# A four-layer convolution chain on one core: order of the set-up, one background task, and the final output by columns

## The chip, the cores and the metric

The kernel runs on one core of a Trainium2 chip. A core has a matrix engine (TensorE, PE in the profile), a vector engine (VectorE, DVE), a scalar engine (ScalarE, ACT), a general engine (GpSimd, POOL) and a synchronising engine (SyncE, SP). [...] Data moves between DRAM and on-chip memory by DMA; SP, ACT and POOL issue the transfers, and 16 DMA engines carry them. The metric is the time of one execution on the device in microseconds (us); less is better.

## What is computed

The input x is 1024 samples of 16 x 16 x 16 values (height, width, channels). Four layers follow, each as x + layer(groupnorm(x)):

```python
x = x + _L0_conv_ref(_gn(x), core0, core1, core2)        # one 4096 x 4096 matrix, given by three small cores
x = x + _L1_conv_ref(_gn(x), ...)                        # cellular automaton step: 3x3 depthwise, 48->128->16, mask
x = x + _L2_conv_ref(_gn(x), filters, bias)              # 3x3 convolution
x = x + _L3_conv_ref(_gn(x), ...)                        # cellular automaton step again
```

`_gn` normalises over 8 groups of two channels. In layer 0 the cores are of the form (r, o, i, k); their contraction is the matrix that is applied to each sample. In layers 1 and 3 every pixel goes through 48 -> 128 (relu) -> 16, and a mask from a 3 x 3 maximum of one channel decides what is kept.

## The kernel before

The samples are handled in two chunks of 512 (NB = 512, NCH = 2). Two large on-chip tiles, `XN[0]` and `XN[1]`, hold a chunk each, or parts and scratch rooms. The order of instructions on every engine is the order in which the Python code makes them: nothing is rescheduled.

**Layer 0** is a train of 13 stages (`phases[0]` to `phases[12]`), about 107 us each, with four units of work each. Before its first unit can start, set-up must do the following; all of it stands in the last part of `conv_preact_kernel`, from L2041 on.

- `train_setup` (from L587) loads the cores and copies core 0 into a widened tile `c0r` (L619, DVE). `sums` (L621) turns that on PE into `A`, and `coefs(0)` makes `R` of it on DVE. `cores` (L631) turns core 1 with PE into the tiles convw and pack.
- `early` (L662) makes the first part of a product g with 64 small matmuls (L644), copies it with ACT (L672) and stores it to DRAM. `keep_g` (L648) issues the stores: two of them in one layout (`g_dram[0]`, L651), and four in another (`g_dram[1]`, L658). `early` calls it for q = 0 and q = 1, all on POOL's queue.
- `gload(0, 1)` and `gload(0, 0)` (L1422, its DMA at L1438) fetch g back for the first unit, from `g_dram[0]` of q = 0. `build(0, 1)` and `build(0, 0)` (L1442) multiply g with R (L1459) and copy the result with ACT (L1464): these are the weights of the first unit. `mix` (L1489) adds halves of them on DVE.
- `input_steps` (from L1053): 8 loads of the input chunk on SP (L1074), statistics on DVE (`stats`, L1086, and `aggregate`, L1116), transposes on PE (L1092) with copies by ACT (L1096, L1098), then `tail`: `root` (L1119, and a square root on ACT, L1120), `widen(0)` (the mean widened by four copies, L1134), `newton` (L1124 to L1128), `widen(1)`. `spread0` and `spread1` turn the widened tiles on PE and copy them with ACT (L1143).
- `kept(0)` and `kept(1)` (L1145) store the turned input to DRAM on POOL (L1151 and L1148).
- `first_normed` (L1176) applies mean and scale to a quarter of the part; `x00`, `x11`, `x10`, `x01` are its four operations each, at L1174. `x00` reads from a tile `raw`; `x11` and `x10` overwrite the tile that `kept(1)` stores. `combined` (L1186, its operations at L1203) makes sums of them.

[...]

**Work beside the train.** `run` places background steps among the pieces of a stage: a span (steps, lo, hi) says from which to which share of the stage. `aside` lists them: stage 7 has `set3`, the preparation of layer 3's weights, with the bound 0.85. Its last steps store a scratch room in `XN[0]` to DRAM (L328 to L330), and the room is written again by the sums for stage 8 (L1203).

**The last layer** of the last chunk is `layer_nca` with `xo`. For every quarter q of the channels and every pair of columns w2 it does matmuls (L1974), relu on ACT (L1977), matmuls (L1803), then `finish` and `residual` on DVE (L1815, L1855, L1860), and after a few slots `turn` (L1864), which transposes on PE (L1867) and copies into `xo` with DVE (L156). At q = 3 the last two column pairs are done in two halves of the samples (hf 0 and 1). SP fetches, two units ahead, the weights `wq` (L1754) and the residual `res` (L1777); for the last pairs their place in SP's order is after the turn of (3, 3). When (q, w2) = (3, 7) is turned, for each half, four stores of 1 MB leave on SP (L1882). Beside it `output_steps(0)` writes the first chunk's output (L1360, L1371).

Of the kernel before, what the change touches and what calls it, by code (L numbers as in the profile page):

```python
# [20 lines left out]
B, S, C = 1024, 16, 16  # L21
P = 128
NB = 512
# [82 lines left out]
def conv_preact_kernel(ctx: ExitStack, tc: tile.TileContext, a: dict, out: bass.AP):  # L106
    nc = tc.nc
# [25 lines left out]
    def work(shape, tag, name, dt=F32):  # L133
        p, sizes = pool["sb"]
        return p.tile(shape, dt, tag=tag, name=name, bufs=sizes[tag])
# [454 lines left out]
    def train_setup(room):  # L590

        c1s = room[:, 0:1024].rearrange("p (h x r k) -> p h x r k", h=2, x=4, r=4)
        c1t = [t[:, 0:512].rearrange("p (x m) -> p x m", x=4) for t in (convw, pack)]
        c1n = work([P, 2, NB], "t4", "core1")[:, :, 0:256]
        r = work([P, NB], "n", "cores")
        c2 = r[:, 0:256]
        c0n = r[:, 256:288].rearrange("p (t k) -> p t k", t=2)

        c0r = work([P, NB], "s", "core0")[:, 0:256].rearrange("p (t n k) -> p t n k", t=2, n=8)
        nc.sync.dma_start(
            c0n, a["L0_conv_core0"].rearrange("r o i k -> (r o i) k").rearrange("(t p) k -> p t k", p=P)
        )
        for g in range(4):
            nc.sync.dma_start(
                c2[32 * g : 32 * g + 16], a["L0_conv_core2"].rearrange("r o i k -> r (o i k)")
            )
        core1 = a["L0_conv_core1"].rearrange("k o i q -> o k (i q)")
        for wv in range(4):  # L610
            for a2 in range(2):
                r0 = 64 * (wv // 2) + 32 * a2 + wv % 2
                (A if wv < 2 else G).dma_start(
                    c1n[r0 : r0 + 31 : 2],
                    core1[8 * a2 + wv : 8 * a2 + wv + 5 : 4].rearrange("h k f -> k h f"),
                )
        G.memset(room[:, 0:1024], 0.0)
        for t in range(2):
            V.tensor_copy(c0r[:, t], c0n[:, t].unsqueeze(1).broadcast_to([P, 8, S]))  # L619

        def sums():  # L621

            t = st0["A"] = work([P, 2, P], "A", "A")
            pt = bank([P, 2, P], "o", "pc0")
            for e in range(2):
                T.transpose(pt[:, e], c0r[:, e].rearrange("p n k -> p (n k)"), ident)
            pt = pt.rearrange("p e (o b i) -> p b i e o", b=2, i=8)
            for b in range(2):
                A.copy(t[:, b].rearrange("p (i e o) -> p i e o", e=2, o=8), pt[:, b])

        def cores():  # L631
            for h in range(2):
                G.tensor_copy(
                    c1s[:, h, :, :, 0:16], c1n[:, h].rearrange("p (x r k) -> p x r k", x=4, r=4)
                )
            for h in range(2):
                pt = bank([P, 4, P], "o", "pc1")
                for x in range(4):
                    T.transpose(pt[:, x], c1s[:, h, x].rearrange("p r k -> p (r k)"), ident)
                A.copy(c1t[h], pt)  # L640

        def gmul(pg, h, ih, x, r, q):
            rows = slice(32 * r, 32 * r + 16)
            T.matmul(  # L644
                pg, c1t[h][rows, 2 * ih + x], c2[rows, 64 * q : 64 * q + 64], start=True, stop=True
            )

        def keep_g(h, q, g, queue):  # L648

            for w in range(2):  # L650
                queue.dma_start(  # L651
                    g_dram[0][h, q, w].rearrange("o s k (t f) -> (s k t) o f", t=2),
                    g[64 * w : 64 * w + 64],
                )
            for w in range(2):
                for v in range(2):
                    rows = slice(64 * w + 32 * v, 64 * w + 32 * v + 32)
                    queue.dma_start(  # L658
                        g_dram[1][v, q, w, :, h].rearrange("o k (t f) -> (k t) o f", t=2), g[rows]
                    )  # L660

        def early():  # L662

            g = work([P, 2, 8, P], "w0", "gw")
            pg = [bank([P, 2, 4, 64], "w", "pg") for _ in range(4)]
            for x in range(2):
                for k in range(4):
                    for r in range(4):
                        gmul(pg[r][:, x, k], 0, k % 2, x, r, k // 2)
            for q, x, r in product(range(2), range(2), range(4)):  # L670
                f = 64 * x + 16 * r
                A.copy(  # L672
                    g.rearrange("p q (o i) f -> p q i o f", i=2)[:, q, :, :, f : f + S],
                    pg[r][:, x, 2 * q : 2 * q + 2].rearrange("p i (o j) -> p i o j", j=S),
                )
                if (x, r) == (1, 3):
                    keep_g(0, q, g[:, q].rearrange("p (o i) f -> p o (i f)", i=2), G)

        def piece(q, h, r0):
            g = flats[0][:, 15360:16384].rearrange("p (o i f) -> p o i f", o=4, i=2)  # L680
            pg = [bank([P, 2, 2, 64], "w", "pg") for _ in range(2)]
            for x in range(2):
                for ih in range(2):
                    for r in range(2):
                        gmul(pg[r][:, x, ih], h, ih, x, r0 + r, q)
            for x in range(2):
                for r in range(2):
                    f = 64 * x + 16 * (r0 + r)
                    A.copy(
                        g.rearrange("p o i f -> p i o f")[:, :, :, f : f + S],  # L690
                        pg[r][:, x].rearrange("p i (o j) -> p i o j", j=S),
                    )
            if r0 == 2:
                keep_g(h, q, g.rearrange("p o i f -> p o (i f)"), nc.sync)

        rest = [
            [(0.6, lambda q=q, h=h, r0=r0: piece(q, h, r0)) for q in qs for r0 in (0, 2)]
            for h, qs in ((0, (2, 3)), (1, (0, 1, 2, 3)))
        ]
        return sums, cores, early, rest  # L700
# [360 lines left out]
    def input_steps(n, tag, queue):  # L1061
# [68 lines left out]
        def widen(k):  # L1130
            st["e", k] = e = work([P, NB], "s", "wide").rearrange("p (g f) -> p g f", g=4)
            src = st["mv"][:, :, :, 0] if k == 0 else st["r"]
            for bg in range(4):
                V.tensor_copy(  # L1134
                    e[:, bg].rearrange("p (w g i) -> p w g i", w=8, i=2),
                    src[:, bg].unsqueeze(1).unsqueeze(3).broadcast_to([P, 8, 8, 2]),
                )
# [585 lines left out]
    def layer_nca(X, n, l, L, xo=None):  # L1723
# [139 lines left out]
        def turn(q, w2, r, hf):  # L1863
            g0, n = (0, 4) if hf is None else (2 * hf, 2)  # L1864
            pt = psum([P, 4, 4, 2, S], "ptx")[:, 0:n]
            for bg in range(n):
                T.transpose(  # L1867
                    pt[:, bg].rearrange("p c v h -> p (c v h)"), r[:, bg * P : bg * P + P], ident
                )
            for v in range(2):  # L1870

                evac(
                    xo[:, g0 : g0 + n, :, 2 * w2 + v, 4 * q : 4 * q + 4].rearrange(
                        "p g h c -> p g c h"
                    ),
                    pt[:, :, :, v],
                )
            if (q, w2) == (3, 7):
                for h in range(0, S, 8):
                    for g in range(g0, g0 + n):  # L1880
                        b0 = NB + g * P
                        nc.sync.dma_start(  # L1882
                            out[b0 : b0 + P, h : h + 8].rearrange("b h w c -> b (h w c)"),
                            xo[:, g, h : h + 8].rearrange("p h w c -> p (h w c)"),
                        )

# [141 lines left out]
    def now(steps):  # L2030
        for step in steps:
            step = step[1] if isinstance(step, tuple) else step
            if callable(step):
                step()
# [5 lines left out]
    with ExitStack() as es:  # L2040
# [5 lines left out]

        A.activation(work([P, NB], "n", "warm")[:, 0:1], ident[:, 0:1], AF.Sqrt)
        (coefs, gload, build, mix), phases = layer_train()
        now([sums])
        coefs(0)  # L2050
        now([cores] + stat[0])
        early()
        gload(0, 1, queue=G)
        gload(0, 0, queue=G)
        now(lines[0])
        kept(0)
        kept(1)
# [5 lines left out]
        mix(0, "s2")  # L2063
        now([spread0] + tail[2:] + [spread1])
        x00, x11, x10, x01 = (first_normed(*at) for at in ((0, 0), (1, 1), (1, 0), (0, 1)))
        now(x00[0::2] + x00[1::2])
        mix(0, "s5")
        now(x11[:2])
        tag[0] = "m"
# [36 lines left out]
        for i in range(4):  # L2106
# [6 lines left out]
        aside = {  # L2113
            2: (set1, 0.85),
            6: (fold1, 0.92),
            7: (set3, 0.85),
            8: (conv_weights(rooms[1]), 0.9),
            9: (fold3, 0.92),
            10: (ahead([(0, 0), (0, 1), (0, 2), (0, 3), (1, 0), (1, 1)], root, rooms[1]), 0.96),
# [4 lines left out]
        for j in range(2, NP - 1):  # L2124
# [3 lines left out]
            n = share.get(j, 0)  # L2128
# [73 lines left out]
```

## Time and profile before

| | us |
|---|---|
| median of 3 runs | 2742.24 (2740.66 to 2749.79) |
| the profiled execution | 2746.07 |
| its span, first to last instruction | 2744.3 |
| PE busy in it | 2675.8 |
| DVE / ACT / POOL busy | 1994.9 / 1241.4 / 541.3 |
| DMA moved | 502.17 MB, mean 183 GB/s |

The profile is of one execution. A line of the timeline has the start and the length in us, the engine (a q behind it: the engine's queue, which issues a DMA), the source line, the operation, the tiles (out<-in), how many instructions are put together, and in brackets how long the engine was idle before it and what ended this. A line of the windows has the stretch, its length, the busy time of PE, its weight loads (PEld), DVE, ACT and POOL with their counts, the granted clock of PE as a share of full speed, the mean busy share of the 16 DMA engines and the GB/s that they moved. A line of the DMA issues has the size of one and the median time from issue to landing.

### The profile page before, as it was taken

To read this page: it belongs to the slowest core of one execution; us is meant where nothing else is said; L and a number is where in the kernel's file an instruction comes from. 1 tells how busy PE (TensorE), PEld (TensorE's weight loads), DVE (VectorE), ACT (ScalarE), POOL (GpSimd) and SP (SyncE) were. 2 spreads that over 40 slices of the span, in tenths; PEclk is the share of its full clock that TensorE was granted. 3 is DMA by queue.
4 is the path that set the end of the run, shared out by engine and by line. 5 is a ranking of instruction groups with operands and counts; after the bars stand their busy time and mean duration, and the time that the engine had idled before them with its cause. 6 is when DMAs were issued, how large, how long until landed. Compare 5 with 4: busy or idle time off the path is not lost.

```text
span 2744.3 us, 47734 instructions
## 1 busy us (share of the span) xinstructions
PE 2675.8 (98%) x19246; PEld 1756.9 (64%) x19246; DVE 1994.9 (73%) x2416; ACT 1241.4 (45%) x2091; POOL 541.3 (20%) x690
## 2 busy tenths in 40 slices
PE   6999999999999999999999999999999999999997
PEld 5888888888888878888778733333333333334344
DVE  8597667867787766667887777658778858756654
ACT  3324222222232222333332276776767756676664
POOL 2000351312122742311331111111113221110000
PEclk8999999999999999999999999999999999999998
DMA  7686788997897687889689764555575866444665
GB/s 254 215 317 227 242 169 214 236 221 188 193 242 193 154 187 180 226 229 263 171 188 257 148 165 102 108 159 122 106 195 83 202 150 143 101 89 116 180 175 209
DMA packets 264796, 502.17 MB, mean 183 GB/s; under 512 B 32804, under 2 KB 100440, under 8 KB 255360
## 3 DMA queue, kind: packets, MB, share of 16 engines
q1 hardware_dynamic: 180752, 338.78, 37.1%
q0 software_dynamic: 83632, 160.22, 33.9%
q8 instruction: 152, 2.49, 0.4%
q14 instruction: 68, 0.56, 0.1%
q10 hardware_dynamic: 192, 0.13, 0.0%
HBM read 280.66 MB, written 223.35 MB: 184 GB/s over the span
## 4 chain that ended last, share of the span: by engine, by line
PE 81%; DVE 8%; DMA 5%; issue 3%; POOL 1%; ACT 1%; SPq 0%; DVEq 0%; POOLq 0%; ACTq 0%
PE po L1567 37%; PE ph L1974 21%; PE po L1803 8%; PE po L1658 5%; PE pw L1459 4%; DMA xn<-in_x_dram 1%; PE po L1667 1%; DVE xn L1174 1%; DMA xf<-r 1%; DMA xn<-xf 1%; DVE xn L1203 1%; PE ptx L1867 1%; DMA L_conv_kp<-xn 1%; DMA xb<-xn 0%; DMA xn<-xn 0%
## 5 line engine op out<-in xcount | busy, mean ns | idle before, releaser
L1977 ACT ACTIVATE hid<-ph,pack 128x512 f32<-128x512 f32 (+1 forms) x1040 | 641.3, 684 | 313.5 <-PE ph L1974 254.3
L1567 PE MATMUL po<-xn,s 128*128 128x256 f32 x3328 | 756.7, 384 | 13.6 <-DVE s L1489 7.2
L1567 PEld LDWEIGHTS po<-xn,s 128*128 128x128 f32 x3328 | 628.5, 191 | 117.5 <-issue 16.7
L1567 PE MATMUL po<-xn,w 128*128 128x256 f32 x2496 | 565.0, 381 | 1.4 <-DVE xn L1203 1.4
L1974 PE MATMUL ph<-xn,wq 32*128 32x512 f32 (+1 forms) x3752 | 518.3, 590 | 1.9 <-DVE u L1815 1.5
L1567 PEld LDWEIGHTS po<-xn,w 128*128 128x128 f32 x2496 | 468.2, 190 | 74.1 <-issue 5.9
L1464 ACT COPY w<-pw 128x512 f32<-128x512 f32 x416 | 213.6, 600 | 454.6 <-PE pw L1459 371.8
L1974 PEld LDWEIGHTS ph<-xn,wq 32*128 32x128 f32 x3752 | 233.6, 184 | 228.9 <-issue 210.0
L1974 PE MATMUL ph<-xn,pack 32*128 32x512 f32 x1288 | 274.2, 607 | 5.6 <-DVE u L1815 1.6
L1489 DVE TENSOR_TENSOR s<-w 128x1024 f32<-128x1024 f32 x208 | 251.2, 1217 | 28.1 <-PE po L1567 24.8
L1803 PE MATMUL po<-hid,pack 128*32 128x512 f32 (+1 forms) x2080 | 256.0, 592 | 0.8 <-ACT hid L1977 0.5
L1815 DVE SCALAR_TENSOR_TENSOR u<-po,pack,xn 128x512 f32<-128x512 f32 (+1 forms) x130 | 96.3, 741 | 168.2 <-PE po L1803 167.1
L1857 POOL DMA_DIRECT2D xf<-u x96 | 82.6, 860 | 618.7 <-DVE u L1855 592.1
L754 DVE TENSOR_TENSOR xn<-xn,m 128x1024 f32<-128x1024 f32 x128 | 150.2, 1217 | 34.7 <-ACT m L777 34.6
L1974 PEld LDWEIGHTS ph<-xn,pack 32*128 32x128 f32 x1288 | 115.6, 184 | 90.7 <-issue 63.1
L1803 PEld LDWEIGHTS po<-hid,pack 128*32 128x32 f32 x2080 | 53.9, 109 | 174.9 <-ACT hid L1977 86.3
L1658 PE MATMUL po<-xn,convw 128*128 128x512 f32 x368 | 163.6, 598 | 0.0
L1203 DVE TENSOR_TENSOR xn<-xn 128x1024 f32<-128x1024 f32 x130 | 152.7, 1215 | 8.0 <-DMA L_conv_kp<-xn 8.0
L1459 PE MATMUL pw<-R,gq 32*128 32x128 f32 x3328 | 143.7, 286 | 7.5 <-DVE small L1116 6.9
L1603 DVE TENSOR_TENSOR r<-r,po 128x1024 f32<-128x1024 f32 x78 | 95.0, 1218 | 72.9 <-PE po L1567 61.0
L1459 PEld LDWEIGHTS pw<-R,gq 32*128 32x128 f32 x3328 | 116.2, 188 | 41.9 <-issue 38.6
L1541 POOL DMA_DIRECT2D xf<-xn x69 | 89.8, 1776 | 251.2 <-DVE xn L1534 71.7
(229 smaller groups left out, 2784.9 us busy)
## 6 DMA issues: line engine op xcount, KB each, us to landing
xn<-xf SPq DMA_DIRECT2D x128, 512.0 KB
xn<-xb SPq DMA_DIRECT2D x36, 1024.0 KB
wq<-L_conv_wy SPq DMA_DIRECT2D x192, 192.0 KB
xf<-xn POOLq DMA_DIRECT2D x69, 512.0 KB, 10.8
piece<-xb SPq DMA_DIRECT2D x64, 512.0 KB
xf<-r POOLq DMA_DIRECT2D x48, 512.0 KB, 12.7
xf<-u POOLq DMA_DIRECT2D x96, 256.0 KB, 4.2
gq<-g_dram SPq DMA_DIRECT2D x94, 256.0 KB
```

The source lines that it names most:

```text
L754: V.tensor_tensor(part, part, m().unsqueeze(1).broadcast_to([P, 2, NB]), op)
L1203: V.tensor_tensor(out, y, z, f)
L1459: T.matmul(pw[r][:, v, i], g[rows, P * (2 * v + i) : P * (2 * v + i) + P], R[rows, k], start=k == 0, stop=k == len(gs) - 1,)
L1464: A.copy(w.rearrange("p b s t m -> p (b s t) m")[:, :, 32 * r : 32 * r + 32].rearrange("p k (v o) -> p v k o", v=2), pw[r].rearrange("p v ...
L1489: V.tensor_tensor(t.rearrange("p s t m -> p (s t m)"), x, y, f)
L1567: T.matmul(po[:, i], matrix(u, what)[:, i, t], x, start=t == 0, stop=t == 3)
L1603: V.tensor_tensor(part, part, po.unsqueeze(2).broadcast_to([P, 2, 2, 256]), ALU.add)
L1658: T.matmul(st["po", h][wh], conv["fw"][:, y], X[:, 16 * wh + h + y - 1], start=y == max(0, 1 - h), stop=y == min(2, S - h),)
L1803: T.matmul(po[32 * j : 32 * j + 32], nca["w1"][:, v], hid[j], start=v == 0, stop=v == 1)
L1815: V.scalar_tensor_tensor(u, po, nca["b1"], X[:, 8 * q + w2, cols(hf)], ALU.add, ALU.add)
L1974: T.matmul(ph, w, x, start=k == 0, stop=k == len(tiles) - 1)
L1977: A.activation(h, ph, AF.Relu, bias=nca["bt"][:, r : r + 1])
```

## The change

Six edits, all of order or placement; the arithmetic is the same.

1. The statistics of the first load stand ahead of everything else on DVE; `cores` goes ahead of `sums`; the copies into `c0r` move into `sums`.
2. `keep_g` can issue its first two stores or its last four alone. `early` issues the first two of q = 0, then both fetches of g, then the other four of q = 0, then the six of q = 1.
3. The widening of the mean for the first chunk goes from DVE to ACT.
4. The operations of `x00` are in their plain order: first half (subtract, multiply), then second half, where before both subtractions stood first.
5. `set3` ends at 0.75 of stage 7 in place of 0.85.
6. The last chunk's output goes by columns: after (3, 3) columns 0 to 7 (rows of 512 bytes), after (3, 5) columns 8 to 11, after each half of (3, 7) columns 12 to 15 (rows of 256 bytes).

```diff
         G.memset(room[:, 0:1024], 0.0)
-        for t in range(2):
-            V.tensor_copy(c0r[:, t], c0n[:, t].unsqueeze(1).broadcast_to([P, 8, S]))
 
         def sums():
 
+            for t in range(2):
+                V.tensor_copy(c0r[:, t], c0n[:, t].unsqueeze(1).broadcast_to([P, 8, S]))
...
-        def keep_g(h, q, g, queue):
-
-            for w in range(2):
+        def keep_g(h, q, g, queue, first=True, second=True):
+
+            for w in range(2 * first):
                 queue.dma_start(
                     g_dram[0][h, q, w].rearrange("o s k (t f) -> (s k t) o f", t=2),
                     g[64 * w : 64 * w + 64],
                 )
-            for w in range(2):
+            for w in range(2 * second):
...
                 if (x, r) == (1, 3):
-                    keep_g(0, q, g[:, q].rearrange("p (o i) f -> p o (i f)", i=2), G)
+                    gs = g[:, q].rearrange("p (o i) f -> p o (i f)", i=2)
+                    keep_g(0, q, gs, G, second=False)
+                    if q == 0:
+                        then()
+                        keep_g(0, q, gs, G, first=False)
+            keep_g(0, 1, gs, G, first=False)
...
-                V.tensor_copy(
+                (A.copy if n == k == 0 else V.tensor_copy)(
                     e[:, bg].rearrange("p (w g i) -> p w g i", w=8, i=2),
...
-            if (q, w2) == (3, 7):
-                for h in range(0, S, 8):
-                    for g in range(g0, g0 + n):
-                        b0 = NB + g * P
-                        nc.sync.dma_start(
-                            out[b0 : b0 + P, h : h + 8].rearrange("b h w c -> b (h w c)"),
-                            xo[:, g, h : h + 8].rearrange("p h w c -> p (h w c)"),
-                        )
+            if q == 3 and w2 in (3, 5, 7):
+                w = slice({3: 0, 5: 8, 7: 12}[w2], 2 * w2 + 2)
+                for g in range(g0, g0 + n):
+                    b0 = NB + g * P
+                    nc.sync.dma_start(
+                        out[b0 : b0 + P, :, w].rearrange("b h w c -> b h (w c)"),
+                        xo[:, g, :, w].rearrange("p h w c -> p h (w c)"),
+                    )
...
-        now([sums])
+        now(stat[0][:1] + [cores, sums])
         coefs(0)
-        now([cores] + stat[0])
-        early()
-        gload(0, 1, queue=G)
-        gload(0, 0, queue=G)
+        now(stat[0][1:])
+        early(lambda: (gload(0, 1, queue=G), gload(0, 0, queue=G)))
...
-        now(x00[0::2] + x00[1::2])
+        now(x00)
...
-            7: (set3, 0.85),
+            7: (set3, 0.75),
```

More of the change, by code (lines that the diff above doesn't have):

```diff
@@ L660, in keep_g, with early @@
                     )
-        def early():
+        def early(then):
             g = work([P, 2, 8, P], "w0", "gw")
```

## The prediction

> **What bounds the kernel now.** The page comes first: TensorE (PE) is busy for nearly the whole span, so only its idle stretches and what lies after its last work can be won or lost.
>
> ```profile
> span 2744.3 us, 47734 instructions
> PE 2675.8 (98%) x19246; PEld 1756.9 (64%) x19246; DVE 1994.9 (73%) x2416; ACT 1241.4 (45%) x2091; POOL 541.3 (20%) x690
> ```
>
> About 68 us without PE: some 47 in set-up and the first pieces, 16 behind the last transpose, the rest in small holes. I then read the timelines of these places, engine by engine. Set-up:
>
> ```profile
> 24.05 0.56 POOL L658 DMA_DIRECT2D g_dram<-gw  x1 [4.21 <-DMA g_dram<-gw]
> 29.03 0.57 POOL L1438 DMA_DIRECT2D gq<-g_dram  x1 [0.69 <-DMA g_dram<-gw]
> 33.34 0.89 POOL L1148 DMA_DIRECT2D xr<-xn  x1
> 33.67 2.09 PE L1459 MATMUL pw<-R,gq 32*128 32x128 f32 x32 [6.89 <-DVE small L1116]
> 41.47 0.26 ACT L1120 ACTIVATE small<-small 128x32 f32<-128x32 f32 x1
> 43.60 4.62 DVE L1174 TENSOR_TENSOR xn<-xn 128x1024 f32<-128x1024 f32 x4
> 49.27 9.66 DVE L1174 TENSOR_TENSOR xn<-xn 128x1024 f32<-128x1024 f32 x8
> ```
>
> POOL's stores of g wait for older stores, so the fetch of g is issued at 29.03 and 30.25; the first build starts at 33.67, when that fetch is in (the named releaser, VectorE, had nothing to give: the build reads R and gq alone). The root (L1120) stands behind the build's eight copies on ScalarE, and the normalisation behind the root. From 43.6 to 77 the chain of waits runs through VectorE (DVE). Its eight operations from 49.27 write into the tile that POOL's store of 33.34 reads, and this store takes long:
>
> ```profile
> xr<-xn POOLq DMA_DIRECT2D x1, 2048.0 KB, 14.5
> ```
>
> 33.34 + 14.5 = 47.8: it is in 1.4 us before DVE wants to write. That slack is all that set-up can give. Stage 7 of 13 has the second place, a store of set3 that holds DVE:
>
> ```profile
> 980.71 17.50 DMA L_conv_kp<-xn
> 998.30 1.23 DVE L1203 TENSOR_TENSOR xn<-xn 128x1024 f32<-128x1024 f32 x1 [8.01 <-DMA L_conv_kp<-xn]
> 999.58 1.99 PE L1567 MATMUL po<-xn,s 128*128 128x256 f32 x8 [2.53 <-DVE xn L1203]
> ```
>
> The end, with SyncE's queue (SP) first:
>
> ```profile
> 2696.60 5.58 SPq L1754 DMA_DIRECT2D wq<-L_conv_wy  x2
> 2702.27 0.38 SPq L1777 DMA_DIRECT2D res<-xf  x1
> 2721.34 11.27 SPq L1882 DMA_DIRECT2D out_dram<-xn  x8
> 2702.32 1.03 DVE L156 COPY xn<-ptx 128x256 f32<-128x256 f32 x2
> 2707.86 2.49 PE L1974 MATMUL ph<-xn,wq 32*128 32x256 f32 x38
> 2727.80 0.58 DVE L156 COPY xn<-ptx 128x128 f32<-128x128 f32 x2 [0.53 <-PE ptx L1867]
> ```
>
> The last weights (wq) and the last residual are asked for at 2696.60 to 2702.27. The copies at 2702.32 are the turn of (q, w2) = (3, 3). PE's group at 2707.86 reads the first of those two wq from its tenth matmul on, 2707.86 + 9 x 0.07 = 2708.5. Rates of the 16 DMA engines, from windows (last two columns: DMA share, GB/s):
>
> ```profile
> 1094.00:1095.00 1.00, 1.00 (x7) 0.87 (x6) 1.00 (x2) 0.00 (x0) 0.00 (x0) 1.00 1.31 214
> 2651.20:2653.00 1.80, 1.80 (x18) 0.42 (x16) 0.00 (x0) 1.19 (x2) 0.00 (x0) 1.00 1.06 263
> 2729.00:2741.00 12.00, 0.00 (x0) 0.00 (x0) 0.00 (x0) 0.00 (x0) 0.00 (x0) 0.52 1.01 420
> ```
>
> The first holds packets of 144 bytes (10.8 ns each on an engine: 144 x 16 / 214), the second nearly all of 512 bytes (943 packets in 1.8 us: 30.5 ns), the third the final stores of 8 KB. So DVE's last copy ends at 2728.4, and the end is set by 8.4 MB of output: 20.0 us at 420 GB/s from 2721.34 + 0.9 to 2742.2, and 2.1 us to close.
>
> [...] the eight input loads of SP come in one behind another, and statistics wait for single ones (DVE idle before 17.32, 23.98). [...] the granted clock is 0.50 in the windows 30 to 47 us, and 32 matmuls pw take 2.09 us there against 1.17 at 64.74.
>
> **The change, part by part.**
>
> *Set-up, early half.* The first statistics now stand ahead of c0r's copies on DVE, and on PE the 2 transposes of sums stand ahead of the 64 matmuls of early. They start when input 0 is in (the trace's semaphore record: 8.9), last 2.65 (8 of 0.33), then copies 0.35, transposes 0.66: early starts at 12.65 in place of 9.71, and the first stores of g leave at 18.1 in place of 15.17. 2.9 us lost. DVE's waits for coefs (1.0) now fall among the statistics, which end at about 35 (33.9 before): hidden by the build.
>
> *Fetch of g behind two stores instead of twelve.* The stores land 8.6 and 9.5 us after issue before, beside the input; with ten fewer beside them I take 9 for the second: 27.7. The fetches go out then, [...] about 2.9 us each to landing (core loads of 32 KB: 2.3): 30.6, against 33.5. Build, root and normalisation come 3 us sooner, or 4.8 if PE keeps its clock. The move of widen(0) to ScalarE puts 4 copies (about 0.22 each) behind the root and mr's first half 1.0 later; the plain order of x00 lets the first matmul go after two operations in place of three. First matmul of the first mix: about 43 in place of 47.14; DVE at x11 at 46 to 47 in place of 49.27.
>
> *What is late next.* The ten stores moved behind the fetches all stand ahead of kept(0) and kept(1) on POOL: from 28.9, ten issues of 0.55 to 0.63, then two of 0.9: kept(1) leaves at 36.3 in place of 33.34. The 4 MB of kept and two fetches of SP took 12.6 us of packets; from 36.5 that gives 49.1, with 1.2 to land 50.3. DVE waits there: 1.0 later than 49.27. Bounds: -2.3 (kept lands by 47) and +3. I take **+1**.
>
> *set3 to 0.75.* Its last stores come up to 0.10 x 107 = 10.7 us sooner, held by POOL's own waits; DVE needs 8. PE's holes there are 2.53 + 0.36 + 0.64. Bounds 0 and -4.3 (with the 0.79 at 995.05); I take **-3**.
>
> *Output by columns.* Before: 8 stores of 1 MB in rows of 8 KB. Now: 4 of 1 MB in 512-byte rows after w2 = 3, 4 of 0.5 MB in 256-byte rows after w2 = 5, 2 and 2 after the halves of w2 = 7: 8192 + 16384 packets in place of 1024. In the built order the first four stand on SP ahead of the last two wq and the last res, which were free to go at 2696.60. SP waits for the copies (2703.35), so the wq are issued after 2705.8, behind 4.19 MB; the two last stores of the first chunk's output wait there too, and nobody waits for them. The res is wanted only at 2719.4 plus the shift. Data from 2704.3; 15.9 us at 263 GB/s gives 2720.2, wq 0.6, landing 0.5: 2721.3. PE waits from 2708.5: 12.8 us, and 2.0 for the half clock after it. Bounds of the wait: 6.8 (at 420 GB/s), 14. Everything later moves by 14.8: copies of w2 = 5 from 2714.5 to 2729.3, of the halves from 2721.3 to 2736.1 and from 2728.4 to 2743.2. A 256-byte packet: 16.6 ns by the line through 144 and 512 bytes, if nothing is added; 30.5 if it costs as much as one of 512; I take 24, 12.3 us for 2 MB. Data: 2730.2 + 12.3 = 2742.5, half 2748.6, half 2754.7, close 2.1: 2756.8, **+12.5**. With 16.6 the last half waits for its copies: 2744.1 + 4.2 + 2.1 = 2750.4, +6.1; with 30.5 it is +19.
>
> Sum: +1 - 3 + 12.5 = +10.5 on a span of 2744.3. That execution took 2746.1, 0.14% above the median of the runs, 2742.24; the difference goes onto the median: **2752.5**.
>
> **Rivals.**
> 1. *Held, but cheap.* The 512-byte stores run at 420 GB/s and those of 256 at 16.6 ns. PE is held 6.8 + 1.5, the last half is out at 2736.7 + 0.9 + 4.3 + 2.1 = 2744.0; sum -0.3 + 1 - 3: 2740. For it: nothing else moves data there. Against: no window of 512-byte rows came near 420.
> 2. *Not slower: the loads are not held.* [...] If the wq pass the stores they land by 2707.7 (1.9 from issue), before 2708.5, and PE ends as before. Then stores from 2704.3: 15.9, another store 1.6, then 8.5, 4.3, 4.3 and 2.1 give 2741.0: -3.3 + 1 - 3: 2737. It decides from the point where the load's data comes within 3 us of issue. Against: inputs that landed in turn.
> 3. [...] 61 ns for 256 bytes (twice 512): 2730.2 + 31 + 16 + 16 + 2 = 2795, +51: 2790. [...]
>
> **How the numbers follow.** Forecast 0.55, its own range 2746 to 2761 (the bounds 16.6 and 30.5, with stage 7 and set-up); rival 1 0.18, rival 2 0.16, rival 3 0.11. 0.3% is 8.2 us, about what a measurement can tell from none. Slower than 2750.5: three quarters of the forecast and rival 3, 0.52. Faster than 2734: a quarter of rival 1, with the better bounds of set-up, and 0.6 of rival 2, 0.14. Between: 0.34. The range 2738 to 2768 leaves out half of rival 2, most of rival 3.
>
> **What would show it.** In the timeline: wq issued after 2705 and PE idle some 12 us near 2708 on a DMA of wq; a granted clock under 1 after it; the final 256-byte stores at about 170 GB/s. In set-up: gq issued at 27 to 28, the root at 37 to 38.5, DVE at x11 waiting for xr<-xn. In stage 7: no DVE wait for L_conv_kp. Wrong if PE has no such wait, or if 256-byte stores pass 300 GB/s.

## The result, and the profile after

| | before | after |
|---|---|---|
| median of the runs taken together, us | 2743.43 (2740.66 to 2749.79, 6 runs) | 2754.86 (2752.45 to 2756.17, 6 runs) |
| the profiled execution, us | 2746.07 | 2754.73 |
| its span, us | 2744.3 | 2753.0 |

The ratio after to before is 1.0035, 95% interval 1.0023 to 1.0047: the kernel became slower, by 6.3 to 12.9 us, about 9.6 (the two medians are 11.4 apart).

The page of after, its span, its first line of busy times and the group of the last layer's matmuls:

```profile
span 2753.0 us, 47737 instructions
...
PE 2675.4 (97%) x19246; PEld 1757.0 (64%) x19246; DVE 1994.3 (72%) x2412; ACT 1241.9 (45%) x2095; POOL 528.2 (19%) x690
...
L1979 PE MATMUL ph<-xn,wq 32*128 32x512 f32 (+1 forms) x3752 | 519.9, 592 | 13.5 <-DMA wq<-L_conv_wy 11.9
```

PE's work is the same, and the span is 8.7 longer: what was added is idle time. The group's last column shows the largest new piece, 11.9 us in which PE waited for wq; in turn the stretch behind PE's last work is shorter, 10.9 us in place of 16.6. Lines of after stand 5 further down than in the code before. The timelines of its set-up and of stage 7:

```profile
27.91 1.11 POOL L1443 DMA_DIRECT2D gq<-g_dram  x2 [8.90 <-DMA g_dram<-gw]
36.66 0.89 POOL L1153 DMA_DIRECT2D xr<-xn  x1
37.91 0.26 ACT L1125 ACTIVATE small<-small 128x32 f32<-128x32 f32 x1
42.88 3.78 PE L1572 MATMUL po<-xn,s 128*128 128x256 f32 x8 [1.93 <-DVE xn L1179]
51.25 9.67 DVE L1179 TENSOR_TENSOR xn<-xn 128x1024 f32<-128x1024 f32 x8 [4.90 <-DMA xr<-xn]
79.38 2.44 PE L1572 MATMUL po<-xn,w 128*128 128x256 f32 x8 [2.33 <-DVE xn L1208]
894.60 0.50 PE L287 MATMUL L_conv_pt<-ident,xn 128*16 128x128 f32 x3 [1.47 <-DMA xn<-in_L_conv_fc_w_dram]
994.29 2.35 DVE L1208 TENSOR_TENSOR xn<-xn 128x1024 f32<-128x1024 f32 x2
```

The first mix starts at 42.88 in place of 47.14, over four us sooner. But kept(1) (L1153) leaves 3.3 us later than before, and VectorE stands 4.9 us for it. The eight matmuls at 79.38 take 2.44 in place of 1.99 before (at 77.38): the granted clock is 0.50 from 80.78 to 84.20, behind a hole of 2.33. In stage 7 VectorE's wait for L_conv_kp is gone (994.29 has no bracket), and PE has a new wait at L287, a transpose of set3 that needs the load of layer 3's weights. The chain of waits says who held the set-up (start, length, what):

```profile
36.66 14.57 DMA xr<-xn
51.23 0.02 issue
51.25 1.24 DVE xn L1179
```

The timeline of the end, SP's queue first, then PE and DVE:

```profile
2704.38 10.19 SPq L1887 DMA_DIRECT2D out_dram<-xn  x4
2714.66 4.64 SPq L1759 DMA_DIRECT2D wq<-L_conv_wy  x2
2719.35 0.65 SPq L1782 DMA_DIRECT2D res<-xf  x1
2728.88 8.04 SPq L1887 DMA_DIRECT2D out_dram<-xn  x4
2736.96 1.55 SPq L1376 DMA_DIRECT2D out_dram<-xo  x1
2738.61 9.15 SPq L1887 DMA_DIRECT2D out_dram<-xn  x4
2708.86 1.56 PE L1979 MATMUL ph<-xn,wq 32*128 32x256 f32 x18
2722.34 4.27 PE L1979 MATMUL ph<-xn,wq 32*128 32x256 f32 x38 [11.92 <-DMA wq<-L_conv_wy]
2742.15 0.58 DVE L156 COPY xn<-ptx 128x128 f32<-128x128 f32 x2 [0.53 <-PE ptx L1872]
```

SP issues the four stores in 10.19 us, so the wq behind them are not even issued before 2714.66. PE waits, and the 38 matmuls after it take 4.27, where the group of 38 before took 2.49 (granted clock 0.50 from 2712.46 to 2726.11 here, 1.00 from 2703 to 2720 there). The store of 2736.96 is the last one of the first chunk's output; it comes up again below. The windows (the clock is the third number from the end, then DMA share and GB/s):

```profile
2709.00:2712.00 3.00, 1.41 (x18) 0.95 (x18) 2.93 (x7) 1.24 (x3) 0.00 (x0) 1.00 0.97 290
2715.00:2718.00 3.00, 0.00 (x0) 0.00 (x0) 0.00 (x0) 0.00 (x0) 0.00 (x0) 0.50 0.97 281
2744.00:2748.00 4.00, 0.00 (x0) 0.00 (x0) 0.00 (x0) 0.00 (x0) 0.00 (x0) 0.50 0.87 215
```

In these windows rows of 512 bytes move at 281 to 290 GB/s and rows of 256 at 215; rows of 8 KB moved at 420 in the kernel before.

To place each gain and loss, I took the start of the same VectorE operation (counted from the last one) in each trace, less that of the kernel before. The first four columns are such shifts at points of the kernel before; "tail" is the difference of the spans less the shift at 2700. All in us:

| trace | at 190 | at 880 | at 1100 | at 2700 | tail | stage 7 (1100 less 880) |
|---|---|---|---|---|---|---|
| after | 3.64 | 3.64 | 0.08 | 0.99 | 7.7 | -3.56 |
| e1_old_output | 3.65 | 3.60 | -0.12 | -0.17 | 0.1 | -3.72 |
| e2_columns_only | -0.32 | 0.45 | -4.68 | -5.12 | 7.1 | -5.13 |
| e3_columns_on_pool | 2.55 | 3.51 | -0.03 | -0.78 | 3.0 | -3.54 |
| e4_kept_first | -2.11 | -1.53 | -4.89 | -6.46 | 7.9 | -3.36 |
| e5_setup_only | 3.42 | 3.84 | -1.30 | -2.75 | 0.0 | -5.14 |
| e6_set3_only | -0.01 | 0.54 | -2.99 | -2.89 | 0.1 | -3.53 |
| e7_loads_on_pool | 2.60 | 4.34 | 1.08 | 0.00 | 0.5 | -3.26 |
| e8_three_fixes | -1.37 | -1.26 | -4.60 | -5.92 | -5.0 | -3.34 |
| e9_early_first | -3.39 | -3.41 | -6.97 | -8.28 | -5.0 | -3.56 |
| e10_early_085 | -3.74 | -2.45 | -1.57 | -1.51 | -4.9 | +0.88 |
| e11_rows_512_held | 1.55 | 1.96 | -1.86 | -2.55 | 9.5 | -3.82 |

After against before by the traces: set-up +3.6, stage 7 -3.6, later stages +0.9, tail +7.7. Each row is one execution. The six traces with the set-up of after (after, e1, e3, e5, e7, e11) lie between 1.55 and 3.65 at 190, so differences of about 2 us between two rows can be those of executions.

### The profile page after: what moved, and what is told of

It is laid out like the page before. It is cut to its first block, busy times and chain, and to the rows that moved or that the text cites. A ratio compares the mean times of both kernels' runs of the same rounds, so it can differ in the third digit from the quotient of the medians.

```text
span 2753.0 us, 47737 instructions
## 1 busy us (share of the span) xinstructions
PE 2675.4 (97%) x19246; PEld 1757.0 (64%) x19246; DVE 1994.3 (72%) x2412; ACT 1241.9 (45%) x2095; POOL 528.2 (19%) x690
## 3 DMA queue, kind: packets, MB, share of 16 engines
q8 instruction: 152, 2.49, 0.4%
## 4 chain that ended last, share of the span: by engine, by line
PE 82%; DVE 8%; DMA 5%; issue 3%; SPq 1%; ACT 1%; POOL 0%; DVEq 0%; ACTq 0%; POOLq 0%
PE po L1572 39%; PE ph L1979 21%; PE po L1808 8%; PE po L1663 5%; PE pw L1464 4%; DMA xn<-xf 1%; PE po L1672 1%; DVE xn L1179 1%; DVE bn L1091 1%; DMA m<-means 1%; PE ptx L1872 1%; DVE xn L1208 1%; DMA xr<-xn 1%; DVE u L1820 1%; DMA xb<-xn 0%
## 5 line engine op out<-in xcount | busy, mean ns | idle before, releaser
L1979 PE MATMUL ph<-xn,wq 32*128 32x512 f32 (+1 forms) x3752 | 519.9, 592 | 13.5 <-DMA wq<-L_conv_wy 11.9
## 6 DMA issues: line engine op xcount, KB each, us to landing
xf<-r POOLq DMA_DIRECT2D x48, 512.0 KB, 12.1
```

The costliest lines, as they stand in the source:

```text
L1979: T.matmul(ph, w, x, start=k == 0, stop=k == len(tiles) - 1)
```

## Experiments

Every ratio below is to runs of the kernel before on the same chip; 0.001 is 2.7 us.

### One edit at a time

**e1_old_output**: edit 6 undone.

```diff
-            if q == 3 and w2 in (3, 5, 7):
+            if (q, w2) == (3, 7):
+                for h in range(0, S, 8):
...
```

> The changed kernel with edit 6 undone: the final output again as eight stores of 8-KB rows after (3, 7). Theory A (the output by columns costs some 8 to 10 us, set-up about +3.6, set3 about -3.5, which cancel): within 3 us of the kernel before (+1), no wait of PE for wq near 2708. Theory B (set-up and its half clock carry the loss, the output little): still 8 us or more above the kernel before.

Measured: 1.0002 (0.9994 to 1.0010), tail 0.1. This is theory A: without the columns nothing of the loss is left, since the other parts cancel in this trace (3.6 at 190, -3.7 in stage 7).

**e2_columns_only**: edit 6 on the kernel before.

```diff
-            if (q, w2) == (3, 7):
...
+            if q == 3 and w2 in (3, 5, 7):
+                w = slice({3: 0, 5: 8, 7: 12}[w2], 2 * w2 + 2)
...
```

> The kernel before with edit 6 alone. Theory A: 8 to 11 us above the kernel before, PE waits 11 to 13 us for wq near 2708 with half clock after it. Theory B: within 2 us of it.

Measured: 1.0025 (1.0017 to 1.0032), that is 4.7 to 8.8 us; PE waits 11.75 for wq, tail +7.1. This is theory A, but about 6.9 us lie under its 8 to 11. One thing was not expected: this trace has the bound 0.85, and it loses next to nothing in stage 7. Its timeline:

```profile
992.85 1.22 DVE L1203 TENSOR_TENSOR xn<-xn 128x1024 f32<-128x1024 f32 x1 [2.11 <-DMA L_conv_kp<-xn]
```

VectorE waits 2.11 where the prediction's profile had 8.01, and PE has no hole there.

**e5_setup_only**: edits 1 to 4 on the kernel before (after, with edits 5 and 6 undone).

```diff
...
-            7: (set3, 0.75),
+            7: (set3, 0.85),
```

> The kernel before with edits 1 to 4 alone (set-up). Theory E: set-up costs 3 to 5 us against the kernel before, with kept(1) landing near 51 and VectorE waiting for it at x11; the first chain of PE past 77 us starts 2 later, and the next stage is at half clock. Rival F: set-up is worth nothing in most executions (the traces' 3.6 us is chance): within 1.5 us of the kernel before.

Measured: 1.0013 (1.0002 to 1.0024), 0.5 to 6.6 us, about 3.6; shift 3.42 at 190. VectorE waited 4.72 us for kept(1), until 52.77. The trace shows theory E, but for the half clock: the shift does not grow after 80 here, while it grows by 1.7 between 80 and 110 in after and in e1. The interval of the times alone would leave room for rival F.

**e6_set3_only**: edit 5 on the kernel before.

```diff
-            7: (set3, 0.85),
+            7: (set3, 0.75),
```

> The kernel before with edit 5 alone (set3 at 0.75). Theory G: no VectorE wait for L_conv_kp in stage 7; that wait was 8.0 us in the profile of the kernel before and 2.1 us in that of e2_columns_only with the same bound 0.85, so the gain differs between executions: median 2 to 4 us lower, and the spread of the times smaller than the 12 us of the kernel before. Rival H: the wait is long in few executions only: median within 1 us, upper end lower.

Measured: 1.0006 (0.9998 to 1.0014), -0.5 to +3.8 us; 13 runs from 2742.34 to 2747.87, where 45 of the kernel before went from 2739.76 to 2753.7. This is nearer to rival H: no gain in the median, and a lower upper end. The trace shows both sides of the edit: there is no wait for L_conv_kp, but PE waits 1.50 us at L287.

### The tail: order, queue or row length

**e3_columns_on_pool**: the column stores on POOL.

```diff
-                    nc.sync.dma_start(
+                    G.dma_start(
                         out[b0 : b0 + P, :, w].rearrange("b h w c -> b h (w c)"),
```

> The changed kernel with the column stores on POOL's queue in place of SP's; the same bytes in the same short rows. Theory A1 (the loss is the order on SP: two wq stand behind 4 MB of stores): wq is issued near 2697 and PE does not wait; last transposes near 2728; the stores run 15.9 + 19.4 us from 2705 on, end at about 2743 to 2745 by the trace, 8 to 10 us under the changed kernel and within 2 of the kernel before. Theory A2 (the loss is the time of 24576 short packets, whatever PE does): no PE wait either, but the end stays at 2750 to 2754.

Measured: 1.0008 (1.0001 to 1.0015), 7.4 under after by the ratios; tail +3.0 in place of +7.7. There is no wait for wq, and the last copy is at 2727. Yet the trace ends at 2746.5. So it lies between the two theories: with PE free most of the loss is gone, but the output on POOL ends no sooner than before. Whether the queue or the rows do this, e3 can't tell; e7 keeps the stores on SP.

**e7_loads_on_pool**: the stores stay on SP, the last loads go to POOL.

```diff
-                nc.sync.dma_start(
+                (G if xo is not None and (q, w2) == (3, 7) else nc.sync).dma_start(
                     st["wq", m],
...
-            nc.sync.dma_start(r, tile_cw(xf[n], i))
+            (G if xo is not None and i == 31 else nc.sync).dma_start(r, tile_cw(xf[n], i))
```

> The changed kernel with the last two wq and the last res issued by POOL, which has nothing else to do there; all stores as in the changed kernel, on SP. Theory A1: no PE wait at wq, and SP's own rates (4.19 MB of 512-byte rows at 263 to 282 GB/s, 4.19 MB of 256-byte rows at 216) end the output at 2741 to 2743 in the trace: 9 to 12 us under the changed kernel, and under e3_columns_on_pool. Theory A2 (short rows cost the same on either queue, as in e3, where the stores ran on to 2745): 5 to 7 us under the changed kernel.

Its timeline, POOL and then SP:

```profile
2696.87 0.58 POOL L1759 DMA_DIRECT2D wq<-L_conv_wy  x1 [222.92 <-DMA xs<-xf]
2702.41 0.56 POOL L1759 DMA_DIRECT2D wq<-L_conv_wy  x1 [4.96 <-PE ph L1979]
2703.39 10.75 SPq L1887 DMA_DIRECT2D out_dram<-xn  x4
```

The same stores of SP go out as in after, but the loads are ahead of them, and PE does not wait. Measured: 1.0008 (1.0001 to 1.0014), 7.4 under after; span 2744.8, tail 0.5. The loads' place behind the stores is the cause of the wait, shown with bytes, rows and the stores' queue unchanged. (Two wq and one res were moved.) The expected 9 to 12 was too much: with rows of 256 bytes the output ends where the eight late stores of 8-KB rows end it (e1's tail is 0.1).

**e11_rows_512_held**: after with no rows of 256 bytes, the loads still held.

```diff
-            if q == 3 and w2 in (3, 5, 7):
-                w = slice({3: 0, 5: 8, 7: 12}[w2], 2 * w2 + 2)
+            if q == 3 and w2 in (3, 7):
+                w = slice({3: 0, 7: 8}[w2], 2 * w2 + 2)
```

> The changed kernel with columns 8 to 15 in one go after each half of (3, 7), rows of 512 bytes, loads still behind the first stores on SP. Theory (the held loads make the last copies late, 2742 to 2743, and what comes after them is nearly the same bytes: 2.1 MB at 288 GB/s, 7.3 us): end at 2751 to 2754 in the trace, within 2 us of the changed kernel, though no row of 256 bytes is left. Rival (the 256-byte rows are the larger loss, as the step from e7 to e8 may suggest): 4 us or more under the changed kernel.

Measured: 1.0041 (1.0028 to 1.0053), not told apart from after; PE waits 12.11 us. The theory holds: while the loads are held, longer rows give nothing that these runs can show.

### The set-up, and a version faster than both

**e4_kept_first**: ten stores of g behind kept.

```diff
-                    keep_g(0, q, gs, G, second=False)
+                    if q == 0:
+                        keep_g(0, q, gs, G, second=False)
                     if q == 0:
                         then()
-                        keep_g(0, q, gs, G, first=False)
-            keep_g(0, 1, gs, G, first=False)
+                        gs0 = gs
+            def rest_of_g():
+                keep_g(0, 0, gs0, G, first=False)
+                keep_g(0, 1, gs, G)
+            return rest_of_g
...
         kept(0)
         kept(1)
+        rest_of_g()
```

> The changed kernel with the ten stores of g that stand behind the two fetches moved behind kept(0) and kept(1) on POOL. Theory C (the ten stores hold kept(1), and its landing holds VectorE 4.9 us at x11): kept(1) is issued at 31 and lands at 46, DVE's wait for xr<-xn near 46 to 51 is gone, the first matmuls after it come 3 to 5 us sooner: 3 to 6 us under the changed kernel. Rival D (the stores only change places: the second unit's fetch of g, which needs them, or a landing of kept that is bound by the DMA engines keeps the time): DVE's wait stays or PE gets a hole near 65, within 2 us of the changed kernel.

The timeline of POOL and VectorE:

```profile
31.52 0.89 POOL L1158 DMA_DIRECT2D xr<-xn  x1
47.16 9.66 DVE L1184 TENSOR_TENSOR xn<-xn 128x1024 f32<-128x1024 f32 x8
```

Kept(1) leaves at 31.52, POOL's own wait for an xr store ends at 45.91, and VectorE goes on at 47.16 without a wait. Measured: 1.0009 (1.0001 to 1.0017), 7.1 under after by the ratios; the shift at 190 is -2.11 in place of 3.64. This is theory C, with 5.8 us in the trace at the upper end of its 3 to 6. The second unit's fetch of g came only at 48.26 and held nobody.

**e8_three_fixes**: the edits of e4, e7 and e11 together, against after.

```diff
+        rest_of_g()
...
+                (G if xo is not None and (q, w2) == (3, 7) else nc.sync).dma_start(
...
+            if q == 3 and w2 in (3, 7):
```

> The changed kernel with kept ahead of ten of the stores of g (e4), the last loads on POOL (e7), and columns 8 to 15 in one go after each half of (3, 7), rows of 512 bytes, so that no row has 256. If the parts add: 6 from set-up, 10 from the loads, 2 from the longer rows, 15 to 19 us under the changed kernel and 6 to 10 under the kernel before. If set-up's gain is given back in a later stage or the output is bound elsewhere: within 3 us of the kernel before.

Measured: 2736.75 against 2743.7, ratio 0.9974 (0.9965 to 0.9983). That is 16.7 under after by the ratios, within the expected 15 to 19. The parts do not simply add, though: longer rows gave nothing alone (e11), and here, with the loads out of the way, the tail falls from 0.5 (e7) to -5.0. One window of e8 in the last stores, with rows of 512 bytes, and one of e7 with rows of 256:

```profile
2724.00:2728.00 4.00, 0.00 (x0) 0.00 (x0) 0.00 (x0) 0.00 (x0) 0.00 (x0) 0.50 0.98 284
```

```profile
2738.00:2742.00 4.00, 0.00 (x0) 0.00 (x0) 0.00 (x0) 0.00 (x0) 0.00 (x0) 0.50 0.88 216
```

At these two rates the later 4.19 MB take 14.8 us in e8 and 19.4 in e7 (an estimate). One other thing differs: SP issued the last store of the first chunk at 2727.61 in e7, between the two groups of four stores (2717.78 and 2730.09), and in e8 ahead of the one group of four (by 2713.52; the group from 2715.43).

**e9_early_first**: e8 with early ahead of sums.

```diff
-        now(stat[0][:1] + [cores, sums])
-        coefs(0)
-        now(stat[0][1:])
+        now(stat[0][:1] + [cores])
         rest_of_g = early(lambda: (gload(0, 1, queue=G), gload(0, 0, queue=G)))
+        now([sums] + stat[0][1:2])
+        coefs(0)
+        now(stat[0][2:])
```

> e8_three_fixes with early's 64 matmuls ahead of the two transposes of sums on PE, and coefs behind the second statistics on VectorE. If the order early behind sums costs what the prediction took (2.9 us at the stores of g) and the chain through the stores sets the first build: stores of g leave 2 to 3 us sooner after PE's start, root and first mix too, time 2 to 3 us under e8. If VectorE's statistics, which end at 35, or the input loads set the root instead: within 1 us of e8.

The timelines of POOL and PE in e9:

```profile
13.82 1.27 POOL L651 DMA_DIRECT2D g_dram<-gw  x2 [7.07 <-ACT gw L672]
24.24 1.11 POOL L1448 DMA_DIRECT2D gq<-g_dram  x2 [9.14 <-DMA g_dram<-gw]
6.46 1.97 PE L639 MATMUL pc<-ident,xn 128*128 128x128 f32 x8 [6.46 <-POOL xn L633]
```

Counted from PE's first matmul, the stores of g leave after 13.82 - 6.46 = 7.4 us; in e8 18.62 - 8.19 = 10.4. So the order costs 3.1 us at the stores, as the prediction had it (2.9). Not all of it reaches the end: from the issue of the first fetch to ScalarE's first copy of the build (L1474) e9 takes 7.6 us (24.24 to 31.80), e8 5.2 (28.73 to 33.90). Median 2733.04 against 2742.99, ratio 0.9966 (0.9954 to 0.9979): 2.2 under e8 by the ratios, 3.7 by the medians, and the intervals overlap. It has the lowest median of the study.

**e10_early_085**: e9 with set3 at 0.85.

```diff
-            7: (set3, 0.75),
+            7: (set3, 0.85),
```

> e9_early_first with set3 at 0.85. Theory (0.75 trades a wait of VectorE for L_conv_kp that few executions show against 1.3 to 1.8 us of PE at L287 in all): median equal or up to 1.5 us lower than e9, no PE wait near 890, and a wider spread, the slowest several us above the median. If 0.75 had removed a wait that most executions have: 3 us or more above e9.

Its timeline in stage 7:

```profile
996.53 1.23 DVE L1213 TENSOR_TENSOR xn<-xn 128x1024 f32<-128x1024 f32 x1 [8.68 <-DMA L_conv_kp<-xn]
```

Measured: 0.9975 (0.9965 to 0.9985), eight runs from 2732.04 to 2739.82, where six of e9 went from 2732.0 to 2735.79. The median is 2.8 above e9, against the theory's "equal or up to 1.5 us lower", but the intervals overlap. The spread is wider, as expected, though eight runs against six do not settle that. This traced execution, 2739.57 us, has the long wait, and PE holes of 1.48 and 2.51 at it.

## Why the prediction was right or wrong

The forecast was 2752.5 (its own sum, 2742.24 + 10.5, gives 2752.7), and the median came out at 2754.86. The direction and the main cause were right. That the total fits so well is partly luck: set-up was put too low, the gain of set3 and the loss of the output too high, and the errors cancel.

*Set-up, forecast +1.* The times up to kept(1) hold: fetches at 27.91 (27.7 forecast), kept(1) leaving at 36.66 (36.3), root at 37.91, first matmul of the mix at 42.88 (43). "What is late next" was named rightly; its size was not. The step that failed is the term "12.6 us of packets ... land 50.3": the store took 14.57, as the row of the DMA issues before had it (14.5), and landed at 51.23. So VectorE at x11 came 2.0 later than 49.27 rather than 1.0 (1.7 to 3.5 in the six traces), and in two traces (after and e1) another 1.7 came between 80 and 110 that the sum did not have; in after the clock was at 0.50 there, from 80.78 to 84.20. Measured alone: +3.6 (0.5 to 6.6). Nor was the slack of 1.4 us "all that set-up can give": with the same store sent sooner, e4 gained 2.1 and e9 3.4.

*set3, forecast -3.* In the one traced pair it was -3.6, and that agreement means little. The step that failed is "DVE needs 8": one execution was taken for all. Four traces with 0.85 show waits of 8.0 (before), 2.1 (e2), 0.3 (e5) and 8.7 us (e10). From the issue of the first store of L_conv_kp to VectorE's next step it was 17.6 us in before (980.71 to 998.30), 14.2 in e2 and 12.9 in e5; why, no run tests. Without the long wait stage 7 is 5.1 us shorter, and then 0.75 is 1.6 us slower: the preparation is pressed into less of the stage, and PE waits for its weights at L287 in seven traces of 0.75 (after, e1, e3, e4, e6, e7, e8: 1.31 to 1.78 us), and not in before, e2 and e5 with 0.85. The sum had no term for that. Measured alone: +1.6 (-0.5 to +3.8), with a smaller spread.

*Output, forecast +12.5.* The mechanism stands: wait 11.92 (12.8 forecast), the clock at 0.50 to 2726.11 (2.0 us for it was the author's estimate; the 38 matmuls took 1.8 more than before), last copies at 2742.7 (2743.2). Some things inside were otherwise. The wait began after eighteen matmuls, at 2710.42, not after nine, and so was shorter. SP did not put the wq behind the stores' data at 2705.8; it was itself at the stores' issues until 2714.66. PE went on at 2722.34, forecast 2721.3, so the sum did not notice. The mis-sized term is the packet of 256 bytes: "I take 24", measured 16.8 mean, 16 median, which is also what the line through 144 and 512 bytes gives when it is worked out again (the prediction has 16.6). The DMA engines were busy for 0.87 of the time (2744 to 2748), and 2 MB took 10.1 and 9.9 us in place of 12.3. The low bound of the prediction gave +6.1, and the tail is +7.7, because a term was put at nothing: "nobody waits for" the first chunk's last store, but its 512 packets ran in the middle of the 256-byte rows, which stood still for 1.5 us (2740.15 to 2741.62).

*Rivals.* Rival 1 needed 420 GB/s from rows of 512 bytes; they had 281 to 290. Rival 2 needed loads that pass the stores; they were not issued before 2714.66, when SP had issued all four, so whether they would pass stays open. Rival 3 took 61 ns for a packet of 256 bytes, an estimate; those of these stores took 16.8, beside 28.9 for 512.

Taken alone the three parts (e5, e6, e2) give 3.6 + 1.6 + 6.9 = 12.1, within the interval measured for all together.

## What to carry to other kernels

Before a store is moved forward on a queue, list the loads that stand behind it there and when their readers want them: here two loads of 192 KB and one of 256 behind 4 MB of stores made nearly all of the tail's 7.7 us, and with the three on an idle engine's queue 0.5 was left. An earlier start of the output paid here with longer rows alone: once the loads were out of the way, it gained 5 us in the tail with rows of 512 bytes (284 GB/s) and nothing with 256 (216). A wait for a store to land, 8.0, 2.1, 0.3 and 8.7 us in four traces of the same stage, should be looked for in a second execution before it is priced from one.

## What was not expected of the hardware

SP was long at issuing its stores of 2048 rows: in after the four issues start at 2704.38, 2704.96, 2708.49 and 2711.39, and the second to fourth take 3.48, 2.86 and 3.17 us, near the 3.6 us that 1 MB takes at the 290 GB/s of the window from 2709 (an estimate). The eight stores with rows of 8 KB in the kernel before took 0.33 to 1.26 us each to issue. POOL issued the same four stores of 512-byte rows in 4.62 us (e3, from 2702.88), where SP took 10.19 (after) and 10.75 (e7). What set the length of an issue was not shown.

Holes of one length were followed by different times. In after PE stood 2.33 us before 79.38, the clock is 0.50 from 80.78 to 84.20, and the eight matmuls after the hole take 2.44. In e4 PE stood 2.34 us before 75.28, and the same eight matmuls take 1.99 and the next eight 1.89. In the kernel before, where the hole was 1.36 us, they took 1.99 with the clock at 1.00. What decides between the two was not shown.
